# Six unread products per group of the slot table, from the first of the group's factors

## The chip, the cores and the metric

One Trainium2 chip, of which the kernel uses one core. The metric is the device time of one execution in microseconds (us); a time given for the kernel is the median of several runs. PE is the matrix engine (PEld its weight loads), DVE the vector engine, ACT the activation engine, POOL the general engine, SP the engine that issues most of the transfers.

## The reference

The input x is [16, 512, 256] in f32. Two branches work on the same normalised x and are multiplied:

```
xn  = layernorm(x)
s   = rwkv_block(xn)          # ln0, ln1, time shift, k/v/r projections, wkv recurrence,
                              # output projection, ln2, channel mix (Wfk, Wfv, Wfr)
probs  = softmax(xn @ Wg)                      # 8192 tokens, 8 experts
sel    = the CAP most probable tokens of each expert
tok2exp = the expert of each token (among those that selected it, else the most probable)
moe = probs[token, its expert] * (gelu(xn @ W1[e]) @ W2[e])     # e = the token's expert
out = x + s * silu(moe)
```

## The kernel before, in words

**Two streams on one core.** The recurrent branch is a generator per sequence b = 0..15 (`recurrent`), cut into nine steps; the list `steps`, written out by hand, says in which order steps of neighbouring sequences are taken. Into this order other work is put at fixed places (`rest_of`): the router over all tokens, the weight loads, the experts (`expert`, in units of 256 tokens), and the outputs. A scheduler then orders the instructions of each engine by priority and by its own idea of what is ready; each engine works its list off in order, and semaphores make it wait for the others. A product of f32 operands shows as two MATMUL records in the trace, one of f16 operands as one.

**Routing.** `route()` finds which expert takes which token. Its last part builds the *slot table*: for each of the slots into which the experts' units are cut, which token it holds. All 64 columns of tokens are handled in four groups of G = 16 (t0 = 0, 16, 32, 48). For each group DVE makes a factor `in_lo` (L477, one-hot over the 128 places within a block, f16, 128 x 2048) and three factors `in_hi` (L483, L487 on DVE, L486 on ACT, f16, 128 x 3 x 78 per column). Then PE adds 16 products `in_lo.T @ in_hi` into one PSUM tile `table` (L492). When all 64 products are in, DVE copies the table out (L497), and makes `holds` (which token a slot holds, L499) and `goes` (where the slot's result goes, L503). The experts' first gathers (`xs`, L751, indirect DMA issued by POOL) need `holds`.

**Around it.** While the table is built, these steps are under way: sequence 3 leaves its first normalisation (`normed`, `shifted`: eight transposes `nps` at L247 on PE, then `hp` at L542 and `mix` at L549 on ACT, L550 on DVE) and goes into its projections k, v, r (L600 on PE, copies L675, L679, L685 on ACT); sequence 2 ends its recurrence (`wkv`, L619 to L638), its output projection `o` (L643, added at L695), its second normalisation (L229, L231 on DVE, L222, L236, L223, L237 on POOL, L239 on ACT) and its channel mix (`mixes`, L561 to L566; the products f at L600; kf at L707 and L708; fr and kv at L643); sequence 4 starts (`x0`, L663, L666, and its statistics). The first expert unit follows: gather `xs`, transposes `xsps` (L757), copy `xsT` (L759), products h (L768), Gelu `act` (L773), products y (L643), copy `ys` (L780), scatter (L782).

**PSUM.** The pool `pp_tr` has two buffers of one bank: the transposes `nps`, `xsps` and those of the routing take turns in it. `pp_mm` has three (k, v, r, f, h), `pp_ot` two (o, fr, kv, y), and `pp_sm` one (`table`).

Of the kernel before, what the change touches and what calls it, by code (L numbers as in the profile page):

```python
# [9 lines left out]
F32 = mybir.dt.float32  # L10
# [9 lines left out]
P = 128  # L20
# [6 lines left out]
def rwkv_times_moe_kernel(ctx: ExitStack, tc: tile.TileContext, a, out: bass.AP):  # L27
# [10 lines left out]
    nc = tc.nc  # L38
    x = a["x"]
    B, T, C = x.shape  # L40
# [17 lines left out]
    pp_tr = ctx.enter_context(tc.tile_pool(name="pp_tr", bufs=2, space=PSUM))  # L58
# [137 lines left out]
    def flat(t):  # L196
        return t.rearrange("p j c -> p (j c)")
# [45 lines left out]
    def transposed(src, h, name):  # L243
# [3 lines left out]
            nc.tensor.transpose(ps[:, j * P : (j + 1) * P], src[:, j, h * P : (h + 1) * P], ident)  # L247
        return ps

# [42 lines left out]
    def route():  # L295
# [20 lines left out]
        ps = pp_tr.tile([P, T], F32, tag="tr", name="ps_pe")  # L316
# [155 lines left out]
        def spread(v, t0, n):  # L472
            return v[:, t0 : t0 + G, None].to_broadcast([P, G, n])

        for t0 in range(0, NT, G):
            in_lo = work.tile([P, G, P], F16, tag="kf", bufs=KF, name=f"in_lo{t0}")
            nc.vector.tensor_tensor(  # L477
                in_lo, spread(lo, t0, P), count_s[:, None, :].to_broadcast([P, G, P]), ALU.is_equal
            )

            in_hi = work.tile([P, G, 3, NS], F16, tag="ex", bufs=2, name=f"in_hi{t0}")
            one, place, seq = (in_hi[:, :, i, :] for i in range(3))
            nc.vector.tensor_tensor(  # L483
                one, spread(hi, t0, NS), count_s[:, None, :NS].to_broadcast([P, G, NS]), ALU.is_equal
            )
            nc.scalar.mul(place, one, place_of[:, t0 // B : t0 // B + 1])  # L486
            nc.vector.tensor_tensor(  # L487
                seq, one, count_s[:, :B, None].to_broadcast([P, B, NS]), ALU.mult
            )
            yield  # L490
            for g in range(G):
                nc.tensor.matmul(  # L492
                    table, lhsT=in_lo[:, g, :], rhs=in_hi[:, g],
                    start=(t0 + g == 0), stop=(t0 + g == NT - 1),
                )
# [439 lines left out]
    for b in steps:  # L935
        if b < 0:
            next(branch[~b])
            continue
        i += 1
        if i == 5:  # L940
            make_mixed()
            routing.append(route())
        next(branch[b])
        if i == 118:
            last_experts()
        if i == 21:
            for _ in routing.pop() if routing else ():
                pass
        for first, last, work_of, n in rest_of:
            for _ in range(n * (i - first) // (last - first), n * (i + 1 - first) // (last - first)):  # L950
                if first <= i < last:
                    next(work_of, None)
# [36 lines left out]
```

## Time and profile before

| | us |
|---|---|
| three runs | 1217.28, 1223.45, 1221.08 |
| median | 1221.08 |
| profiled execution, its own time | 1215.99 |
| its span in the profile | 1214.2 |
| PE busy in the span | 1118.9 (92%) |
| DVE busy | 782.9 (64%) |
| ACT busy | 714.6 (59%) |
| POOL busy | 370.6 (31%) |
| mean granted PE clock | 0.971 of full speed |

The busy shares are means over stages. A line of the timeline gives the start and the duration in us, the engine, the source line, the operation, what it writes and reads, the number of records merged into it (x32), and in brackets how long the engine had been idle before it and which instruction ended the wait. The page's PEclk row and the clock column of a table by stretches give the share of the full clock that PE was granted.

### The profile page before, as it was taken

The page shows a single profiled execution, that of the slowest core. Times are in us where ns is not written, and L with a number is a line of the kernel's source. Part 1 is how long each engine was busy: PE and PEld are TensorE (multiplying, and loading weights), DVE is VectorE, ACT ScalarE, POOL GpSimd, SP SyncE. Part 2 cuts the span into 40 slices and gives each one's busy share as a digit, 9 for nine tenths or more (in the row PEclk, how much of TensorE's full clock was granted, in tenths as well). Part 3 has the DMA queues.
Part 4 walks back from the last instruction along what each step waited for, and adds up shares of the span by engine and source line. Part 5 has one row for each costly group of instructions (what it writes and reads, how often), then busy time and mean ns, then how long its engine had stood idle before and what let it go on. Part 6 is the DMA issues. An engine that isn't in the chain of part 4 may idle for free. (4 is left out here: it accounts for less than half of the span.)

```text
span 1214.2 us, 12759 instructions
## 1 busy us (share of the span) xinstructions
PE 1118.9 (92%) x4333; PEld 770.6 (63%) x4333; DVE 782.9 (64%) x1324; ACT 714.6 (59%) x1158; POOL 370.6 (31%) x479
## 2 busy tenths in 40 slices
PE   4887989579999999999999999999999999899988
PEld 2444646345848768586675857768577685647555
DVE  6888587985572844728457183572736637699954
ACT  4775965347383753928448284582745828576832
POOL 7522020043232514216152251511424112243221
PEclk8998999698999999999999999999999999989989
DMA  7681020232323314223141331413232210878353
GB/s 244 224 295 52 1 104 1 104 112 76 90 70 104 130 61 126 66 90 113 41 139 52 107 102 35 139 57 121 66 104 87 91 65 18 229 171 180 96 104 53
DMA packets 69056, 125.14 MB, mean 103 GB/s; under 512 B 6263, under 2 KB 44173, under 8 KB 68749
## 3 DMA queue, kind: packets, MB, share of 16 engines
q1 hardware_dynamic: 53916, 97.55, 24.1%
q0 software_dynamic: 15072, 26.75, 10.1%
q8 instruction: 35, 0.57, 0.2%
q14 instruction: 33, 0.26, 0.1%
HBM read 90.72 MB, written 41.42 MB: 109 GB/s over the span
## 5 line engine op out<-in xcount | busy, mean ns | idle before, releaser
L600 PE MATMUL f<-mix_k,WfkT_sb 128*128 128x512 f32 x512 | 235.1, 614 | 13.4 <-DVE mix_k L566 13.4
L643 PE MATMUL kv<-WfvT_sb,kf 128*128 128x256 f32 x1024 | 228.8, 380 | 1.7 <-ACT frs L718 0.7
L643 PEld LDWEIGHTS kv<-WfvT_sb,kf 128*128 128x128 f32 x1024 | 193.5, 190 | 29.4 <-ACT frs L718 1.1
L782 POOL DMA_INDIRECT ys_d<-ys,goes x72 | 81.4, 1131 | 400.4 <-ACT ys L780 311.2
L600 PEld LDWEIGHTS f<-mix_k,WfkT_sb 128*128 128x128 f32 x512 | 97.2, 195 | 129.0 <-issue 99.4
L733 DVE SCALAR_TENSOR_TENSOR frs<-frs,kv 128x512 f32<-128x512 f32 x30 | 20.5, 685 | 199.8 <-PE kv L643 199.8
L643 PE MATMUL y<-w,act 128*128 128x256 f32 x576 | 133.6, 380 | 1.3 <-ACT act L773 1.3
L768 PE MATMUL h<-xsT,w 128*128 128x256 f32 x576 | 130.2, 379 | 0.0
L768 PEld LDWEIGHTS h<-xsT,w 128*128 128x128 f32 x576 | 109.4, 190 | 16.6 <-issue 1.9
L643 PEld LDWEIGHTS y<-w,act 128*128 128x128 f32 x576 | 107.1, 190 | 20.3 <-issue 5.3
L637 DVE RECIPROCAL ex<-ex 128x512 f32<-128x512 f32 x32 | 107.2, 3349 | 0.6
L751 POOL DMA_INDIRECT xs<-xn_d,holds x72 | 78.7, 1093 | 79.5 <-PE xsps L757 60.9
L707 ACT ACTIVATE kf<-f 128x512 f32<-128x512 f32 x128 | 74.4, 592 | 33.1 <-PE f L600 32.1
L718 ACT ACTIVATE frs<-fr 128x512 f32<-128x512 f32 x32 | 19.0, 595 | 110.4 <-PE fr L643 110.4
L780 ACT COPY ys<-y 128x512 f32<-128x512 f32 x32 | 18.7, 583 | 97.7 <-PE y L643 97.6
L629 DVE TENSOR_TENSOR_SCAN ba<-ex 128x512 f32<-128x512 f32 x32 | 39.0, 1218 | 56.4 <-ACT ex L628 56.4
L239 ACT ACTIVATE n<-x,nm,rs 128x256 f32<-128x256 f32 x128 | 68.5, 594 | 10.2 <-POOL nm L237 10.2
L643 PE MATMUL o<-WoT_sb,vT 128*128 128x256 f32 x256 | 64.7, 399 | 7.1 <-DVE frs L733 6.0
L708 ACT ACTIVATE kf<-kf 128x1024 f32<-128x1024 f32 x64 | 67.5, 1054 | 1.0
L600 PE MATMUL k<-mix_k,WkT_sb 128*128 128x512 f32 x128 | 62.7, 625 | 5.3 <-DVE mix_k L550 5.3
L773 ACT ACTIVATE act<-h 128x512 f32<-128x512 f32 x72 | 41.8, 597 | 41.4 <-PE h L768 41.1
L643 PE MATMUL fr<-WfrT_sb,mix_r 128*128 128x256 f32 x256 | 60.9, 380 | 1.1 <-ACTq L804 1.1
(223 smaller groups left out, 1894.6 us busy)
## 6 DMA issues: line engine op xcount, KB each, us to landing
w<-in_W_dram SPq DMA_DIRECT2D x72, 512.0 KB, 3.9
xa<-in_x_dram SPq DMA_DIRECT2D x16, 512.0 KB, 4.7
xn_d<-xn SPq DMA_DIRECT2D x16, 512.0 KB, 8.0
out_dram<-in_x_dram SPq DMA_DIRECT2D x15, 512.0 KB, 4.7
xc<-xn_d SPq DMA_DIRECT2D x14, 512.0 KB, 5.0
s_d<-x SPq DMA_DIRECT2D x14, 512.0 KB, 2.6
s<-s_d SPq DMA_DIRECT2D x14, 512.0 KB
out_dram<-s POOLq DMA_DIRECT2D x28, 256.0 KB, 5.9
```

The source lines that it names most:

```text
L239: nc.scalar.activation(dst[:, j, :], src[:, j, :], AF.Identity, bias=nm[:, j : j + 1], scale=rs[:, j : j + 1])
L600: mm = nc.tensor.matmul(ps, lhsT=w[:, h, o * P : (o + 1) * P], rhs=src[:, h, :], start=(h == 0), stop=(h == NC - 1))
L629: nc.vector.tensor_tensor_scan(ba[:, 0, 1:], ex[:, 2, :], ex[:, 0, :], 0.0, ALU.mult, ALU.add)
L637: nc.vector.reciprocal(den, den)
L643: mm = nc.tensor.matmul(ps[:, jj, :], lhsT=lhsT_of(c, j), rhs=w[:, c, :], start=(c == 0), stop=(c == n - 1))
L707: nc.scalar.activation(t[:, o, :], project(wfk, xk2, q * 2 + o, f"f_{b}_{q}_{o}"), AF.Relu)
L708: nc.scalar.activation(t, t, AF.Square)
L733: nc.vector.scalar_tensor_tensor(fr, fr, 1.0, psv, ALU.add, ALU.mult)
L751: nc.gpsimd.indirect_dma_start(out=xs[:, j, :], out_offset=None, in_=xn_d[:, :], in_offset=rows_at(holds, 2 * i + j))
L768: nc.tensor.matmul(ps[:, ff, :], lhsT=w1[:, h, (f + ff) * P : (f + ff + 1) * P], rhs=xsT[:, h, :], start=(h == 0), stop=(h == NC - 1),)
L773: nc.scalar.activation(act, ps, AF.Gelu)
L782: nc.gpsimd.indirect_dma_start(out=ys_d[:, :], out_offset=rows_at(goes, 2 * i + j), in_=y[:, j, :], in_offset=None)
```

## The change

A helper `keep_awake` is added. It takes a tile of `pp_tr` (128 x 512 f32, one bank, of the two) and makes n products into it, each one overwriting the last; nothing reads the tile. It is called once in each of the four groups, with n = 6, right after the group's `in_lo` is made; the products take the first block of `in_lo` as weights and its first four blocks (128 x 512 f16) as the moving operand. What the kernel computes is unchanged. Lines of the changed kernel lie seven further down behind the helper, and eight further down behind the call.

```
+    def keep_awake(n, lhsT, rhs):
+        ps = pp_tr.tile([P, T], F32, tag="tr", name="unread")
+        for _ in range(n):
+            nc.tensor.matmul(ps, lhsT=lhsT, rhs=rhs, start=True, stop=True)
...
         for t0 in range(0, NT, G):
             in_lo = work.tile([P, G, P], F16, tag="kf", bufs=KF, name=f"in_lo{t0}")
             nc.vector.tensor_tensor(
                 in_lo, spread(lo, t0, P), count_s[:, None, :].to_broadcast([P, G, P]), ALU.is_equal
             )
+            keep_awake(6, in_lo[:, 0, :], flat(in_lo[:, : T // P, :]))
 
             in_hi = work.tile([P, G, 3, NS], F16, tag="ex", bufs=2, name=f"in_hi{t0}")
```

## The prediction

> **What bounds the kernel now.** First the page: PE is busy for 92% of the span, and the clock row is at 9 except in a few slices, one of them the eighth (212 to 243 us), where the slot table is built.
>
> ```profile
> PE 1118.9 (92%) x4333; PEld 770.6 (63%) x4333; DVE 782.9 (64%) x1324; ACT 714.6 (59%) x1158; POOL 370.6 (31%) x479
> ...
> PEclk8998999698999999999999999999999999989989
> ```
>
> A table by stretches of 25 us shows PE idle for 0 to 2 us in each from 275 to 1050 us. So PE is the bound behind the table: whatever is left undone for PE when that dense part begins is paid at the end, and whatever PE does in its holes before is free. The holes come from the waits of PE in 219 to 277 us (us in total, times, longest):
>
> ```profile
> PE table L492 <- ACT in_hi L486: 8.4, 1, 8.4
> PE nps L247 <- ACT n L239: 3.7, 1, 3.7
> PE table L492 <- DVE in_hi L487: 3.2, 1, 3.2
> PE xsps L757 <- DMA xs<-xn_d,holds: 2.8, 1, 2.8
> PE f L600 <- DVE mix_k L566: 1.5, 1, 1.5
> ```
>
> The timeline shows what fills the rest, PE first:
>
> ```profile
> 229.52 5.26 PE L492 MATMUL table<-in_hi,in_lo 128*128 128x234 f16 x32 [8.41 <-ACT in_hi L486]
> 238.03 3.30 PE L492 MATMUL table<-in_hi,in_lo 128*128 128x234 f16 x16 [3.25 <-DVE in_hi L487]
> 241.12 3.14 PE L600 MATMUL k<-mix_k,WkT_sb 128*128 128x512 f32 x4
> 244.10 1.79 PE L492 MATMUL table<-in_hi,in_lo 128*128 128x234 f16 x16
> ```
>
> The same product takes 164, 206 and 112 ns: the clock (0.50 in 228 to 231 us, 0.60 in 231 to 234, 0.50 in 237 to 243, 0.90 in 243 to 246). But DVE works without a gap from 220 to 244 us, and it makes the factors:
>
> ```profile
> 223.07 2.29 DVE L477 TENSOR_TENSOR in_lo<-lo,count_s 128x2048 f16<-128x2048 f16 x1
> ...
> 239.92 1.45 DVE L487 TENSOR_TENSOR in_hi<-in_hi,count_s 128x1248 f16<-128x1248 f16 x1
> ...
> 245.93 0.40 DVE L497 COPY of<-table 128x234 f32<-128x234 f32 x1 [1.75 <-PE table L492]
> ...
> 268.21 0.36 DVE L231 BATCH_NORM_AGGREGATE mv<-st 128x2 f32<-128x6 f32 x4
> ```
>
> So a slow clock costs here only the 1.75 us that DVE waits for the last group. The dense part begins with sequence 2's f:
>
> ```profile
> 272.29 2.07 ACT L239 ACTIVATE n<-x,nm,rs 128x256 f32<-128x256 f32 x4 [5.01 <-POOL nm L237]
> 274.27 0.56 ACT L780 COPY ys<-y 128x512 f32<-128x512 f32 x1
> ...
> 276.61 5.09 PE L600 MATMUL f<-mix_k,WfkT_sb 128*128 128x512 f32 x6 [1.51 <-DVE mix_k L566]
> ...
> 281.98 11.32 PE L600 MATMUL f<-mix_k,WfkT_sb 128*128 128x512 f32 x26
> ...
> 287.66 0.60 ACT L239 ACTIVATE n<-x,nm,rs 128x256 f32<-128x256 f32 x1 [0.59 <-POOL nm L237]
> ```
>
> **The change, part by part.**
>
> *The products.* 24 of 512 f16 columns. The table's, of 234 columns, take 112 ns at the faster clock and 206 at the slower; by columns that is 245 to 451 ns, a group of six 1.5 to 2.7 us, all 5.9 to 10.8 us. No row has this shape; I take the slower for groups 0 and 16, the faster behind. Group 0 can start at 223.05 (its in_lo ends), 16 at 225.36: both end by 228.5, in the 8.4 us hole, which lasts to 229.5. Group 32 starts at 233.04 and ends in the second hole; group 48 starts at 236.61 and ends at 238.1 to 239.3, where the table's third group could start at 237.97. Cost 0.1 to 1.3 us on PE, hidden by DVE, whose last factor comes at 241.4; I take 0.
>
> *The table.* At 112 ns the 64 products take 7.2 instead of 10.4 us. The last group is bound by DVE: factor at 241.0 (a 0.4 us x0 now stands before it where a 0.7 us mix stood), products to 242.8, `of` copied at 243.2 instead of 245.9: 2.7 us earlier, and the first gather at 246.1 instead of 248.8.
>
> *What is moved.* The list of each engine in the built kernel differs in one stretch, up to sequence 2's kv, and is the same again behind it. The unread tiles take turns in the transposes' two buffers, and sequence 3's eight transposes, on PE at 219.0 to 221.1 before, now stand after the table's third group, at about 239 to 241. Everything behind them moves: hp and mix on ACT from 219.7 to 225.0 into the time after 240.7, between sequence 2's Relus and its Exp; the six mixes on DVE (0.7 each) from 239 to 252 into 244.7 to 258.5; sequence 4's x0 goes ahead of them. PE does half of k at 245.3, and then waits for the gather (250.2, with 4.1 us from issue to transposes as now). k, v, r at 0.43 us a record and two records a product, and three products of h, take it to 260 (262 if the clock falls, as it did at 255 to 258 us after the 2.8 us hole), then o to 264 (265.6).
>
> *Sequence 2.* DVE has no hole left (1.75 and 2.7 us before) but does one 1.2 us scan more before the statistics; with o at 264 to 265.6, the aggregates end at 266.3 to 268.0 against 268.6. I take 267.2, 1.4 earlier. POOL's chain is 3.7 us as now, so n starts at 270.9 and ends at 272.9.
>
> *The first gain lost on ACT.* Before, expert 0's table load and both Gelu stand before n (260.9 to 263.9), so that y is done by 269.3, in what would be a hole. Now the load (1.28) and one Gelu (0.6) stand after n and before sequence 2's mix_k, which costs 1.3 more than the ys copy (0.56) that went: f starts at 276.2 against 276.6, 0.4 earlier. And of y's 16 records only 4 come before f. The other 12 come after it, at 0.226 us: 2.7 us that PE did in a hole before and does now in the dense part.
>
> *A new wait.* ACT now has sequence 3's Relu and sequence 4's first n before the second kf pair's other half. n waits for POOL (xs3's gathers after xsps1, 2.3 us, then 3.0 us of rs and nm). xsps1 now stands after 12 records of f, not 6. With the clock as before (6 of them at 0.85 us, 6 at 0.43) xsps1 ends at 284.5, nm at 289.9, the kf at 291.0; PE runs out of its three f buffers at 289.6: 1.4 us of stall, and 0.5 at the next, since a square (1.05) and an n stand there too.
>
> *The sum.* -0.4 + 2.7 + 1.9 = +4.2 us when the dense part is in step again. What can lower it is the clock at f: 6 records at 0.85 cost 2.6 us before. If f starts at full clock, xsps1 ends at 282.0 and the sum is about +2. Between +2 and +4.2 I take **+3**, as nothing decides where the clock rises. Against the profiled execution that is 1219 us; that one lies 5.1 us under the median, so for the median I add 3 to 1221.1: **1224 us**.
>
> The transposes at 272.9 to 275.1 us did not raise the clock: 0.72 in 273 to 276, 0.50 in 276 to 279. The Trainium skill, "TensorE: Matmul & The Clock Gate", section "PE-mode transpose", says that transposes do not count as busy for the gate. By it, f would start slow in the changed kernel too, and the sum would be +4.2; by a row-by-row reading alone it stays open.
>
> That page's section "The HAM clock gate" says the gate opens after a busy window of some 3.4 us and closes after an idle one. By it the twelve products from 223 us open it by about 228 us, and the later holes under 3 us need not close it; but an open gate here buys only what the last group costs, 1.75 us on DVE.
>
> **The rivals.**
> 1. *Slower, by the ACT queue.* Same mechanism as the new wait, larger: if o ends later than 265.6 (k, v, r wholly at the slow clock: 24 records at 0.85 instead of 0.43, up to 10 us, of which about 5 are in no hole), the aggregates come past 269, f starts 2 to 4 us later than before, with y still after it: +7 to +10, 1228 to 1231. It decides from 2 us of delay at the aggregates. For it: a hole of 3 us before the gather as now. Against: the clock rose again within 3 to 4 us (0.62 in 255 to 258, 1.00 after).
> 2. *Faster, by the earlier table.* If the first Gelu waits for nothing and PE's clock stays up through 277, f starts 3 us earlier (as the gather does) and nothing stalls: -3 + 2.7 - 2.6 = -3, 1218. For it: the gather and the aggregates do come earlier. Against: ACT's order, fixed.
> 3. *The products do not wake PE* (or it falls asleep again in the 1 us before 229.5): table at 206 ns; its last group ends at 244.3, still before 245.9. All else is order: about +4, 1225.
>
> **How the numbers follow.** Measurement tells 0.5%, 6.1 us, from no change. Forecast (0 to +6 us): 0.67, all within. Slower rival: 0.20, of which 0.18 is past 6.1. Faster rival (-1 to -7): 0.09, of which 0.03 is past the bound. No wake-up: 0.04, within. So faster 0.03, same 0.79, slower 0.18. The range takes the forecast with the runs' own spread (-4, +2 around the median) and most of the slower rival: 1216 to 1231.
>
> **What would show it.** Right: 24 records at 223 to 239 us in holes, table records near 112 ns, `of` near 243 us, sequence 3's hp near 241, a Gelu between n and mix_k, twelve y records behind f, a PE wait for an ACT kf near 290, and every later step shifted by 2 to 4 us. Wrong: f earlier than 275 or later than 278 us, no stall at 290, or a shift that changes after 330 us. The forecast fails most easily at the clock from 252 to 280 us and at ACT's order.

## The result, and the profile after

Eight runs of the changed kernel have a median of 1226.66 us (1224.66 to 1228.53), eight of the kernel before 1220.12 (1217.28 to 1223.45). The ratio is 1.0056, 95% interval [1.004, 1.0071]: 6.5 us slower. The prediction said 1224.0 us, in 1216 to 1231. A later set of six runs gave the same ratio (experiment 0).

The page's PE row and clock row, in the same form as before:

```profile
PE 1129.1 (92%) x4357; PEld 774.2 (63%) x4357; DVE 783.7 (64%) x1325; ACT 713.9 (58%) x1157; POOL 369.6 (30%) x479
...
PEclk9998989788999999999999999999999999999989
```

The eighth slice, which held a 6, has a 7, but the ninth has an 8 where it had a 9; slices of 30 us tell little here. By stretches of 3 us the clock is 0.50 up to 231 us, 0.89 in 231 to 234, 1.00 in 234 to 240, 0.82 in 240 to 243 and 0.62 in 243 to 246, and the table's 64 products take 8.06 us, not 10.35: the table is built at a higher clock. PE is busy for 10.2 us more (1129.1 against 1118.9). Against the profiled execution of before, the one of after (1227.79 us, span 1226.0) is 11.8 us longer, nearly twice what the medians say. So the two traces have to be set against a mark of their own, not against the start. The mark here is DVE's reduction of `ps_one`, the last instruction on DVE's list ahead of the routing's slots, at 212.68 us before and 216.56 after. The 3.9 us ahead of it are no effect of the change, which issues its first instruction behind it: the same four records of sequence 1's f, for one, took 1.96 us in the one execution (at 177.35 us) and 3.76 in the other (at 178.66), and in the experiments below the mark stands at 212.95 to 215.64 us, with the change's edits and without them.

Later on such a thing happens once more, behind a hole of the same length in both. PE's timeline, of before and then of after (start, us, engine, line, operation, count, and in brackets the idle time before and what ended it):

```profile
576.13 14.00 PE L600 MATMUL f<-mix_k,WfkT_sb 128*128 128x512 f32 x32 [1.98 <-DVE mix_k L566]
```

```profile
585.93 15.70 PE L608 MATMUL f<-mix_k,WfkT_sb 128*128 128x512 f32 x32 [1.98 <-DVE mix_k L574]
```

The 32 records took 14.00 us in one execution and 15.70 in the other, behind the same idle time of 1.98 us. These 1.7 us, too, have nothing to do with the change. What the change itself cost is in between. Every row of this table counts from the mark:

| us from the mark | before | after | difference |
|---|---|---|---|
| `of` copied (DVE) | 33.25 | 31.83 | -1.4 |
| first gathered transposes on PE | 40.29 | 38.83 | -1.5 |
| the other three of them | 41.71 | 40.51 | -1.2 |
| sequence 2's aggregates (DVE) | 55.53 | 57.24 | +1.7 |
| sequence 2's f starts | 63.93 | 67.54 | +3.6 |
| f ends | 80.62 | 84.01 | +3.4 |
| sequence 2's kv starts | 86.08 | 92.06 | +6.0 |

From kv on the difference stays at 6.0 for some 270 us, until the f just shown. The 6.0 us are within 0.5 of what the medians say.

PE's waits in 219 to 300 us of after (us in total, times, longest):

```profile
PE xsps L765 <- DMA xs<-xn_d,holds: 3.2, 2, 1.9
PE k L608 <- DVE mix_k L558: 2.5, 1, 2.5
...
PE y L651 <- ACT act L781: 1.2, 1, 1.2
...
PE f L608 <- ACT kf L715: 0.6, 1, 0.6
```

The 8.4 us in which the table waited for ACT's `in_hi` are 1.6 now, and 6.0 us stand as waits of the unread products for `in_lo`. The wait of f for DVE's `mix_k` has gone, and waits of k for `mix_k`, of y for a Gelu and of f for a kf are new. PE's timeline shows the stretch in order:

```profile
227.55 4.77 PE L255 MATMUL unread<-in_lo 128*128 128x512 f16 x12 [3.90 <-DVE in_lo L484]
233.96 3.43 PE L500 MATMUL table<-in_hi,in_lo 128*128 128x234 f16 x32 [1.64 <-ACT in_hi L494]
...
246.56 1.79 PE L500 MATMUL table<-in_hi,in_lo 128*128 128x234 f16 x16
250.87 2.57 PE L608 MATMUL k<-mix_k,WkT_sb 128*128 128x512 f32 x4 [2.52 <-DVE mix_k L558]
255.39 0.44 PE L765 MATMUL xsps<-ident,xs 128*128 128x128 f32 x1 [1.95 <-DMA xs<-xn_d,holds]
257.07 0.90 PE L765 MATMUL xsps<-ident,xs 128*128 128x128 f32 x3 [1.24 <-DMA xs<-xn_d,holds]
257.77 3.62 PE L608 MATMUL k<-mix_k,WkT_sb 128*128 128x512 f32 x4
261.18 4.19 PE L608 MATMUL v<-mix_v,WvT_sb 128*128 128x512 f32 x8
...
284.10 6.40 PE L608 MATMUL f<-mix_k,WfkT_sb 128*128 128x512 f32 x12
...
296.67 3.90 PE L608 MATMUL f<-mix_k,WfkT_sb 128*128 128x512 f32 x8 [0.59 <-ACT kf L715]
300.41 2.75 PE L651 MATMUL y<-w,act 128*128 128x256 f32 x12
```

The 24 unread products stand where PE waited before. Groups 0 and 16 of the table take 107 ns a product (3.43 us for 32), not 164; the third (2.84 us for 16 from 243.12) takes 178, the last 112. Sequence 3's transposes come behind the third group (seven of the eight records at 245.80). Half of k follows 2.5 us after the last group, and PE then waits twice for the gather; the other half of k and all of v come behind it, at 0.9 and 0.52 us a record. The clock in 252 to 261 us was 0.50 to 0.52. Last, 12 of y's 16 records stand behind f.

The timelines of DVE, of POOL and of ACT in the same stretch of after:

```profile
270.58 0.69 DVE L703 TENSOR_TENSOR x<-x,o 128x512 f32<-128x512 f32 x1 [3.40 <-PE o L651]
```

```profile
250.18 1.53 POOL L223 TENSOR_TENSOR r<-r,power 128x4 f32<-128x4 f32 x1
251.92 1.32 POOL L759 DMA_INDIRECT xs<-xn_d,holds  x1 [0.21 <-issue]
```

```profile
278.19 2.08 ACT L239 ACTIVATE n<-x,nm,rs 128x256 f32<-128x256 f32 x4 [3.51 <-POOL nm L237]
280.29 1.28 ACT L781 ACT_TABLE_LOAD   x1
281.58 0.60 ACT L781 ACTIVATE act<-h 128x512 f32<-128x512 f32 x1
282.08 1.44 ACT L571 ACTIVATE mix_k<-nps,cols,cmk 128x511 f32<-128x511 f32 x2
```

DVE waits 3.40 us for o (2.66 before) before it can add it and take sequence 2's statistics. POOL makes r for x0 (four instructions from 249.26, L666 to L223) ahead of the first gather, where it had a copy of 0.96 us before. On ACT, the table load and a Gelu stand between n and `mix_k`, which f needs.

### The profile page after: what moved, and what is told of

The parts are those of the page before. It is cut to its first block, busy times and chain, and to the rows that moved or that the text cites. A ratio compares the mean times of both kernels' runs of the same rounds, so it can differ in the third digit from the quotient of the medians.

```text
span 1226.0 us, 12810 instructions
## 1 busy us (share of the span) xinstructions
PE 1129.1 (92%) x4357; PEld 774.2 (63%) x4357; DVE 783.7 (64%) x1325; ACT 713.9 (58%) x1157; POOL 369.6 (30%) x479
## 5 line engine op out<-in xcount | busy, mean ns | idle before, releaser
L608 PE MATMUL f<-mix_k,WfkT_sb 128*128 128x512 f32 x512 | 239.8, 623 | 12.5 <-DVE mix_k L574 11.9
L759 POOL DMA_INDIRECT xs<-xn_d,holds x72 | 76.2, 1059 | 81.2 <-PE xsps L765 62.3
```

Source lines behind the costliest of these rows:

```text
L608: mm = nc.tensor.matmul(ps, lhsT=w[:, h, o * P : (o + 1) * P], rhs=src[:, h, :], start=(h == 0), stop=(h == NC - 1))
L759: nc.gpsimd.indirect_dma_start(out=xs[:, j, :], out_offset=None, in_=xn_d[:, :], in_offset=rows_at(holds, 2 * i + j))
```

## The experiments

The theory that the traces suggest: the unread products themselves cost nothing; what costs is the order, and it does so at two places, (A) the aggregates, 1.7 us late behind the late transposes, and (B) ACT's queue behind them, where the load and the Gelu ahead of `mix_k` hold f up (1.9 us more from the aggregates to f) and most of y is left for the time behind f (2.6 us). The rivals: that the products cost time on PE; that the clock is what matters; that the late transposes of sequence 3 are the whole price, ACT's order being only a sign of it.

All ratios are to the kernel before, of runs on the same chip, with 95% intervals. "Stretch" is how much later than before kv of sequence 2 starts, counted from the mark: the table's last row.

| kernel | ratio | f starts | stretch |
|---|---|---|---|
| 0: the change again | 1.0056 [1.0039, 1.0074] | +3.9 | +6.4 |
| 1: unread tiles in other buffers | 0.999 [0.9976, 1.0005] | -1.0 | -1.5 |
| 2: order without products | 1.0063 [1.0044, 1.0082] | +6.5 | +9.0 |
| 3: products in two groups only | 1.0074 [1.0054, 1.0094] | +3.8 | +6.1 |
| 4: Gelus behind n, no products | 1.005 [1.0035, 1.0065] | +1.1 | +5.0 |
| 5: change + 4 products at the gather | 1.0059 [1.0039, 1.008] | +4.4 | +6.4 |
| 6: kernel 1 + 4 products ahead of f | 1.002 [1.0004, 1.0035] | -0.1 | +0.1 |
| 7: kernel 6 + 2 ahead of sequence 13's f | 1.0004 [0.9988, 1.002] | +1.0 | +1.1 |
| 8: change + 5 products at the gather | 1.0027 [1.0016, 1.0038] | +3.5 | +1.8 |
| 9: before + 2 ahead of sequence 13's f | 1.0008 [0.9995, 1.002] | -0.9 | -1.4 |

Kernel 9 differs from the kernel before only behind 1060 us, and its stretch came out 1.4 us shorter. So a stretch of a single execution is good to about 1.5 us, and smaller differences in it are not read. It may be the execution of before that is the long one: kernel 1, which has its order too, came out 1.5 us shorter, and sequence 3's r, eight records, took 4.69 us in before, 3.83 in kernel 1 and 3.85 in kernel 9. Then the others cost up to 1.5 us more than the column says.

The aggregates (the fourth row of the table that counts from the mark) are late in every kernel with the late transposes (0, 2, 3, 5, 8: by 1.9 to 4.6 us) and early in every kernel without them (1, 4, 6, 7, 9: by 0.9 to 2.1 us). So place A goes with the transposes.

**0. The change again**, beside experiments 1 to 3.

> The changed kernel once more, on the chip on which the three others run, so that all four stand beside the same runs of the kernel before. All theories: ratio 1.004 to 1.007 to the kernel before, as measured.

Measured: 1226.24 us against 1219.2, ratio 1.0056 as at first. Its profiled execution lost 6.4 us in the stretch, in the same rows as the table (`of` at 31.81, aggregates at 57.49, f at 67.80, kv at 92.44).

**1. The same products, in other buffers.**

```diff
-        ps = pp_tr.tile([P, T], F32, tag="tr", name="unread")
+        ps = pp_mm.tile([P, T], F32, tag="mm", name="unread")
```

With this the lists of DVE, ACT, POOL and SP are those of the kernel before, and PE's is that list with the 24 products put in.

> The unread tiles lie in the pool of the projections (three buffers) instead of that of the transposes (two). The 24 products stay; the lists of DVE, ACT, POOL and SP are those of the kernel before, and PE's differs by the products alone. Order theory (the time came from the moved transposes and what moved behind them, the products lie in holes): no slower than before, ratio 0.997 to 1.000, since the table's records go to about 112 ns and the copy of the table comes 1 to 2 us earlier. Product theory (PE's own time for the products, or what they take from others, is the cost): ratio about 1.0055, as the changed kernel.

Measured: 1218.62 us, ratio 0.999 [0.9976, 1.0005]. The first twelve products take 4.92 us (4.77 in the change) and the table's first 32 the same 3.43, `of` is copied 0.6 us earlier than before, and the whole is not slower. So the products cost at most 0.05%, and what they do for the clock of the table is worth at most 0.24% (the interval's two ends). The rival that they cost time on PE falls.

**2. The order without the products.** Sequence 3's transposes are tied behind the last product of the third group, and nothing is added; the lists are those of the changed kernel without the 24 products, but that all eight transposes stand behind the third group on PE, where the change has one ahead of it.

```diff
+            if t0 == 2 * G:
+                table_mm.append(mm)
...
-            ps = transposed(n, h, f"nps_{name}")
+            with tc.issue_after(table_mm[0].ins) if table_mm and name == "1_3" else nullcontext():
+                ps = transposed(n, h, f"nps_{name}")
```

> No unread product; the eight transposes of sequence 3's first normalisation are held behind the table's third group, which gives all engines the lists of the changed kernel without the 24 products. Order theory: ratio 1.004 to 1.008 to the kernel before, y's 12 records behind f, aggregates 1 to 3 us later than before. Product theory: 0.999 to 1.001. A third theory, that the products waken PE and save something within the bad order: 1 to 2 us slower than the changed kernel, with the table's records at 160 to 206 ns.

Measured: 1227.68 us, ratio 1.0063. Order alone makes the whole difference. With experiment 1 this is the four-way comparison: neither 1, products alone 0.999, order alone 1.0063, both 1.0056. In the stretch of single executions the products even give something back in the bad order (+9.0 without them, +6.0, +6.4 and +6.1 with), but the ratios don't resolve that.

**3. Products in the last two groups alone.**

```diff
-            keep_awake(6, in_lo[:, 0, :], flat(in_lo[:, : T // P, :]))
+            if t0 >= 2 * G:
+                keep_awake(6, in_lo[:, 0, :], flat(in_lo[:, : T // P, :]))
```

> The six products only in the last two of the four groups; the lists of DVE, ACT, POOL and SP are those of the changed kernel, PE's has 12 products fewer. Order theory: ratio 1.004 to 1.007, as the changed kernel, since the order is the same. Product theory: half the cost, about 1.003. The first two groups' records of the table at the slow clock (164 ns and more), the last two's at 112.

Measured: 1227.82 us, ratio 1.0074, stretch +6.1. Its lists are those of the change less 12 products, and it costs as much: no difference to the end shows from what the first two groups' products do to the clock.

**4. ACT's order alone.** The kernel before, with the first unit's Gelus (and so the table load) tied behind the second normalisation of sequence 2. The transposes of sequence 3 stay where they were, and there are no products. The scheduler answers with a little more than that: y's 12 records and the first unit's scatters go behind f, and on DVE sequence 4's x0 changes places with a scan of the same length (1.22 us).

```diff
-            nc.scalar.activation(
+            n_made[name] = nc.scalar.activation(
...
-            nc.scalar.activation(act, ps, AF.Gelu)
+            with tc.issue_after(n_made["2_2"].ins) if i == 0 else nullcontext():
+                nc.scalar.activation(act, ps, AF.Gelu)
```

> The kernel before, with only one thing moved: the two Gelu of the first expert unit are held behind sequence 2's second normalisation n. No unread products, sequence 3's transposes stay early. Theory that the price of the order lies in what follows on ACT (a table load and a Gelu between n and mix_k, y's 12 records behind f): 3.5 to 5 us of the changed kernel's 6 to 7, ratio 1.003 to 1.0045, with f 1.3 to 2 us later after the aggregates and the aggregates not later. Rival, that the price lies in the late k, v and r alone (slow clock, the wait for the gather): ratio 1.000 to 1.001.

Measured: 1224.58 us, ratio 1.005 [1.0035, 1.0065]. The timeline of ACT, then that of PE, in this kernel:

```profile
272.58 2.08 ACT L241 ACTIVATE n<-x,nm,rs 128x256 f32<-128x256 f32 x4 [10.42 <-POOL nm L239]
274.68 1.28 ACT L776 ACT_TABLE_LOAD   x1
```

```profile
292.67 3.90 PE L602 MATMUL f<-mix_k,WfkT_sb 128*128 128x512 f32 x8 [1.12 <-ACT kf L709]
296.41 2.75 PE L645 MATMUL y<-w,act 128*128 128x256 f32 x12
```

Here the aggregates were 1.7 us earlier than before (some 1 us of that is the execution of before, as kernels 1 and 9 show), and still f started 1.1 us later; f waited 1.12 us for a kf, and the 12 y records stand behind it. So place B without A costs nearly as much as the change, with none of the change's edits in the kernel. It is larger here than in the change, though: from the aggregates to f 2.8 us are added (1.9 in the change), and f is 1.4 us longer (0.2 shorter in the change).

**5. PE kept awake ahead of the gather.** The changed kernel, with four unread f32 products into the first gathered transposes' own tile, ahead of them.

```diff
+        if i == 0:
+            for _ in range(4):
+                nc.tensor.matmul(psx.rearrange("p c r -> p (c r)"), lhsT=wk[:, 0, :P], rhs=wfk[:, 0, :T], start=True, stop=True)
```

> The changed kernel, with four more unread f32 products of 128x512 (8 records, 3.4 us at the full clock) from constants, into the tile that the first gather's transposes overwrite afterwards; they stand after the table's last group, in PE's wait before k and for the gather. The lists of the other engines are those of the changed kernel. Theory that the slow clock of k, v and r makes the aggregates late: they come 1.5 to 3 us earlier than in the changed kernel, ratio to the kernel before 1.003 to 1.0045. Rival, that the late gather and DVE set it: ratio as the changed kernel, 1.0056.

Measured: 1226.18 us, ratio 1.0059. It did not do what it was made for: the products ran early (245.6 to 249.2 us), PE still had 2.75 us of hole ahead of the gather, and k behind it was slow again, as this kernel's timeline of PE shows:

```profile
255.11 5.01 PE L608 MATMUL k<-mix_k,WkT_sb 128*128 128x512 f32 x6
```

6 records in 5.01 us are 0.84 each, against 0.43 at full clock. So whether a warm clock here would bring the aggregates forward stays untested.

**6. PE kept awake ahead of f.** Experiment 1's kernel, with four unread f32 products in the first f's tile, tied behind o.

```diff
+        for _ in range({"f_2_0_0": 4}.get(name, 0)):
+            with tc.issue_after(last_o[0].ins):
+                nc.tensor.matmul(ps, lhsT=wk[:, 0, :P], rhs=wfk[:, 0, :T], start=True, stop=True)
```

> The kernel with the unread tiles in the other pool, with four more unread f32 products from constants in the tile of sequence 2's first f, held behind its output projection, so that y moves up to f and PE has no long hole before f. Theory that the slow clock at f costs 2 to 2.6 us: ratio to the kernel before 0.997 to 0.998. Rival: a delay of y and of the transposes eats it, 0.999 to 1.000.

Measured: 1220.98 us, ratio 1.002 [1.0004, 1.0035]: no gain, if anything a loss. PE's timeline of this kernel, at the end of f:

```profile
293.57 1.98 PE L611 MATMUL f<-mix_k,WfkT_sb 128*128 128x512 f32 x4 [1.79 <-ACT kf L718]
```

f does start at full clock: its first 6 records, at 279.15, take 2.74 us, not 5.09. But y, which the scheduler now puts between the transposes and f, holds f up, and PE ends up in a wait of 1.79 us for a kf on ACT, whose queue stands behind an n that waits for POOL. The 2.35 us that the clock gave came back as a wait and a later start. The rival that the clock is what matters falls at this place.

**7. The same, and two more products ahead of sequence 13's f.**

```diff
-        for _ in range({"f_2_0_0": 4}.get(name, 0)):
+        for _ in range({"f_2_0_0": 4, "f_13_0_0": 2}.get(name, 0)):
```

> As the one before, with two more such products before sequence 13's f, in PE's 2.4 us wait. Its 32 records took 15.7 us against 14.0 for sequence 14's. If the clock stays up: 1.7 us less, ratio to the kernel before 0.995 to 0.9965; if the outputs' transfers set the end, no further gain.

Measured: 1220.29 us, ratio 1.0004 [0.9988, 1.002]; the interval overlaps that of experiment 6, so what the two products did can't be told from this run. Experiment 9 takes them alone.

**8. Place B undone, the late transposes kept.** Experiment 5 with five products. This turned the scheduler's order on ACT back (the expectation calls it the planner): load and first Gelu ahead of n.

```diff
-            for _ in range(4):
+            for _ in range(5):
```

> The changed kernel with five more unread products of 512 f32 columns (10 records, some 4.5 us) on PE ahead of the first gathered transposes. The planner's answer to them: sequence 3's transposes stay behind the table's third group, as in the change, but the table load and the first Gelu now stand ahead of n of sequence 2, as before the change, and 14 of y's 16 records ahead of f. So the unread products and the late transposes stay, and ACT's order ahead of f is undone. Theory 1 (the price of the change is what ACT's order costs: 1.9 us more from the aggregates to f and 2.6 us of y behind f, 4.5 us, and 1.7 us of late aggregates): f 1 to 2 us late and 0.5 us of y behind it, so the stretch up to kv of sequence 2 costs 0 to 3 us against before, the ratio 1.000 to 1.003. Theory 2 (the late transposes themselves are the price, by the late mixes and k, v, r): ratio 1.005 to 1.007 as in the change. The clock: the hole ahead of the gather gets shorter by about 0.9 us; if k and v's 16 records take near 7 us instead of 9.2, the aggregates come 2 us earlier.

Measured: 1222.27 us, ratio 1.0027 [1.0016, 1.0038], half of what the change costs, and the interval lies wholly below the change's. The timeline of ACT, then that of PE, in this kernel:

```profile
274.17 0.60 ACT L784 ACTIVATE act<-h 128x512 f32<-128x512 f32 x1
277.20 2.07 ACT L239 ACTIVATE n<-x,nm,rs 128x256 f32<-128x256 f32 x4 [2.43 <-POOL nm L237]
```

```profile
282.07 5.31 PE L608 MATMUL f<-mix_k,WfkT_sb 128*128 128x512 f32 x12
...
296.42 0.59 PE L651 MATMUL y<-w,act 128*128 128x256 f32 x2
```

The unread products of the change are all there, and the transposes of sequence 3 are as late as in it. The aggregates are even later (+3.0 us from the mark, since k and v were slow again and k stands wholly behind the gather), and so f starts as late as in the change. But of y only 2 records stand behind f, f's first 12 records take 5.31 us instead of 6.40 behind 10 records of y, and no kf is waited for: the stretch costs 1.8 us instead of 6. So the late transposes are not the whole price: without the bad order on ACT about half of it goes by the ratios, and 4.2 of 6.0 us by the stretch. The comparison isn't clean, since the five products are in it too and k stands elsewhere. Experiment 4, from the other side, gives B more, 0.50 of the 0.56%; the intervals are too wide for exact shares of A and B.

**9. Two products ahead of sequence 13's f, in the kernel before.** The two products of experiment 7, alone.

> The kernel before with two unread products of 512 f32 columns (4 records, 1.9 us) in the hole of 2.4 us ahead of sequence 13's f, and nothing else; the lists of the other engines are those of before. Before, these 32 records take 15.7 us, against 13.8 at 0.43 us a record. Theory 1 (a hole of 2.4 us costs f part of its clock, and filling it gives it back): f's 32 records in 14.0 to 14.2 us, 1.5 us gained. Theory 2 (the next step waits for something else): PE waits as much longer for DVE's frs ahead of kv, where it waits 0.4 us now, and the time is that of before. Ratio 0.9985 by the first, 1.000 by the second; the interval may hold both, the trace decides.

Measured: 1218.71 us, ratio 1.0008 [0.9995, 1.002]. PE's timeline of this kernel, f and the second kv of sequence 13:

```profile
1078.78 14.16 PE L603 MATMUL f<-mix_k,WfkT_sb 128*128 128x512 f32 x32 [0.54 <-DVE mix_k L566]
...
1105.05 7.17 PE L646 MATMUL kv<-WfvT_sb,kf 128*128 128x256 f32 x32 [1.75 <-DVE frs L736]
```

f took 14.16 us instead of 15.70, and the wait of kv for DVE's `frs` grew from 0.41 to 1.75 us: 1.54 gained, 1.34 given back. The second theory holds. Experiment 1 remains the fastest of all of them, and it can't be told from the kernel before.

## Why the prediction was right, and where it was wrong

The time, 1226.66 us, lies in the stated range. The difference lies at the edge of the forecast (0 to +6 us): +6.0 by the profiled stretch, and just past it by the medians (+6.5), where the prediction had put 0.18, all of it on the first rival. The mechanism was right in kind: no cost of the products, all of it order. The sum held better than its terms, and that is luck: f's start was missed by 4.0 us one way and f's length by 2.1 the other.

| step | predicted, us | measured, us |
|---|---|---|
| unread products on PE | 0 | 0 (experiment 1) |
| `of` copied | -2.7 | -1.4 |
| aggregates of sequence 2 | -1.4 | +1.7 |
| from the aggregates to f | +1.0 | +1.9 |
| f: start | -0.4 | +3.6 |
| f: its length, with its waits | +1.9 | -0.2 |
| y behind f | +2.7 | +2.6 |
| sum | +4.2, taken +3 | +6.0 |

- *The products lie in PE's holes.* Right, by their places in the timeline and by experiment 1.
- *The table.* Right that it runs at 107 to 112 ns and ends earlier, but `of` came half as much earlier: the third group ran at 178 ns a product, and seven transposes stood between it and the last, which started 30.0 us from the mark (242.7 in before's time) and not at 241.0. Some 0.6 us of this was there ahead of the first product: `in_lo` starts 8.65 us from the mark, 8.08 before.
- *Sequence 2's aggregates, 1.4 us earlier.* This step failed, in sign. It took the gathered transposes for ready at 250.2 us of before's time; the last three came at 253.2 (40.51 from the mark), as `of` came 1.3 us later than thought and POOL had its four instructions for r (249.26 to 251.71) in front of the gather, which the step didn't count on POOL's queue. And it gave k, v, r their full clock from there; 4 records of k and 8 of v took 7.8 us where 12 at 0.43 are 5.2. So o ended at 268.0 in before's time, not at 264 to 265.6, and DVE, which the step left no hole, waited 3.40 us for it. The clock was 1.00 in 249 to 252 us and 0.50 to 0.52 in 252 to 261; that it was lost to the holes of 1.95 and 1.24 us is likely but not shown, as the runs that were to show it (5, 8) left a hole there.
- *ACT's order ahead of f.* Right in kind: load and Gelu behind n, 12 records of y behind f. From the aggregates to f 1.9 us were added and not 1.0. About 0.3 of that is the prediction's own arithmetic: aggregates 1.4 us earlier and 1.3 more on ACT make f 0.1 earlier, not 0.4 (its 276.2 leaves out the 0.2 us from ACT's mix_k to f in before's rows). The rest is that the end of the aggregates to n was 4.0 us and not 3.7, and that n to f grew by 1.6 and not by 1.3.
- *The new wait for a kf.* Right that it appears, too large: 0.59 us once, not 1.4 and 0.5. The 12 records of f ahead of the second gathered transposes took 6.4 us, not 7.7: f did start at a slow clock (0.50 in 282 to 285 us), but it rose sooner (0.79 in 285 to 288). The two misses together are enough to explain that f's length didn't grow at all.

What happened is the first rival's course at a smaller size: k and v slow, aggregates past 269 us (269.9 in before's time), f 3.6 us later, y behind it. The rival priced it at +7 to +10 by 5 us of slow clock on PE; 2.6 came. The forecast came near the total from other terms: 4.0 us too little at f's start, 2.1 too much within f. The rival of no wake-up fell by the table's rows, the faster one by the aggregates. Of "what would show it wrong", f came past 278 us (280.2 in before's time), as the forecast itself had said would speak against it.

The Trainium skill, "TensorE: Matmul & The Clock Gate", section "Why this matters for your kernels", advises no idle gaps of PE over some 3 us. In this case a shorter hole was followed by a slow clock too, but not each time: behind the 1.98 us ahead of the f shown above, the clock was 0.50 in 587 to 590 us in the one execution and 1.00 throughout in the other.

## What to carry to other kernels

Filler work can cost more by what it displaces than by what it takes: before adding any, ask which buffers it takes its turn in, and compare each engine's list before and after; here the same 24 products cost 0.56% in one PSUM pool and nothing in another. A faster clock on an engine is worth only what the next waiting engine leaves of it: three times (the table, sequence 2's f, sequence 13's f) PE got 1.5 to 2.4 us faster at one place, and each time another engine set the pace behind it. When an order moves, follow every queue it passes, and ask of each first-needed result what now stands ahead of it, above all a table load and an activation that could have been done in a hole.

## What was not expected of the hardware

The granted clock behind a hole of about 2 us is not the same from one execution to the next, with the same instructions: 14.00 and 15.70 us for the same 32 records behind 1.98 us of idle time, and 1.96 or 3.76 us for the first four records of sequence 1's f. Within one kernel, sequence 13's f took 15.70 us behind a hole of 2.36, and that of the next one 14.00 behind 2.46. The pair of profiled executions so differs by 5.6 us (3.9 and 1.7) without any cause in the code, which is why the stretch was counted from a mark.
